# Layer 1's key and query projection as seven half-size products, and two late loads, in a four-layer transformer kernel on one core

## Chip, core and metric

The kernel runs on one core of a Trainium2 chip. The core has a matrix engine (TensorE: PE, with its weight loads shown as PEld), a vector engine (VectorE: DVE), an activation engine (ScalarE: ACT), a general one (GpSimd: POOL) and a queue engine (SyncE: SP); SP and POOL start the DMA transfers here. The metric is the time of one execution on the device in microseconds.

## The reference

Four residual layers follow each other on x of shape (4, 1024, 256), all in float32: attention A, a feed-forward network, attention B, and the same feed-forward network again.

```python
x = x + attn_a(layernorm(x), kernel, WO)      # layer 1
x = x + ffn(layernorm(x), w1, b1, w2, b2)
x = x + attn_b(layernorm(x), ...)             # low rank, with rotation
x = x + ffn(layernorm(x), w1, b1, w2, b2)

def attn_a(x, kernel, WO):                    # 16 heads of 64
    q, k, v = (einsum('bsm,hmd->bhsd', x, kernel[i]) for i in range(3))
    scores = einsum('bhsd,bhtd->bhst', q, k) * (1 / (64 * 64 * 16))
    out = einsum('bhst,bhtd->bhsd', softmax(scores), v)
    return out.transpose(0, 2, 3, 1).reshape(b, s, 1024) @ WO[0]
```

## The kernel before

Everything is written in a hand-made order. Both attentions share `attention`. Work goes by pairs: a pair is one of 4 batches and one of 8 couples of heads, so there are 32 pairs, and each has 8 steps of 128 query rows, 256 steps in all. In a step s the loop `steps_with` emits, engine by engine in this order: `invert(s)` (the reciprocal of the row sums on DVE, L268, and its copy on ACT, L269); `scores(s + 1)` (PE, L247: eight matmuls into two PSUM tiles j = 0 and 1 of 128x1024); on even steps the pT sends of POOL (L304) and `project` (PE by L176; ACT copies the result as `got`, L335; POOL adds it to x, L337); `exponentials(s + 1, 0)` (row maximum on DVE, L258; exponential with row sum on ACT, L260); the pieces that are due half a step early; on odd steps `weigh` (PE, L313); `exponentials(s + 1, 1)`; on odd steps `take` (ACT copies, L323, POOL's product, L325); `turn(s)` (DVE transposes 32x32 blocks into T, L280); on odd steps the pT sends of SP (L304, eleven per two steps, the POOL queue sends five); and last the pieces due at s.

PSUM has two pools. `ps_sc` has three tiles of 128x1024, which the scores take in rotation, two per step, so that a tile waits for the exponential that reads the one three places before it. `ps_mm` has two banks, which `group` hands out in turn for everything else: projections, values, output projection, weighted sums.

The keys and queries of a pair are made during the pair before. `pair_a` gives the pieces: `qk(i, qb)` makes the keys (i = 1) or queries (i = 0) of 512 rows, by `paired` (L176): two accumulated blocks of the 256 input features, each as two matmuls side by side that fill 64 partitions. Each call takes one bank from `group`, and ACT copies it out (L758 for keys; L756 for queries, with the scale). The four calls lie in the even steps 0, 2, 4 and 6 of the pair before, due half a step early, which puts their ACT copy between the two exponentials of the step. `values(m)` (PE, L185; ACT copy, L769) fills four even steps too. `batch_a` prepares the next batch: normalized rows `xn` (L156), turned by PE against the identity (L162) and copied to `hT` by ACT (L165).

The weights of a pair come by POOL's queue (L742) some five steps before they are used. `load_rest` loads at the start the other batches of x (SP's queue), and by POOL's queue both FFN matrices, biases, the low-rank weights of layer 3 and the rotation's tables (four transfers). The FFN's `weights` makes combinations of w1 (DVE) and w2 (POOL) once per network: its middle blocks use Strassen's scheme already (`up_seven`, `down_seven`), the first and the last block use plain products (`up`, `down`). `rotate` (L870 to L872) reads the tables in layer 3.

Of the kernel before, what the change touches and what calls it, by code (L numbers as in the profile page):

```python
# [15 lines left out]
P = 128  # L16
# [3 lines left out]
NC = D // P  # L20
# [28 lines left out]
def hybrid_block_kernel(  # L49
# [24 lines left out]
    pp, tp, ptp, otp, tmp = pool("p", 2), pool("T", 2), pool("pT", 2), pool("oT", 1), pool("tmp", 1)  # L74
    lowp, highp, xnp, rp = pool("low", 2), pool("high", 1), pool("xn", 1), pool("rope", 1)
    qkp, vp, wp, wop = pool("qk", 2), pool("v", 2), pool("wp", 2), pool("wo", 2)

# [15 lines left out]
    w1_sb = const.tile([P, NC, F], F32, name="w1_sb")  # L93
    w2_sb = const.tile([P, NF, D], F32, name="w2_sb")
    b2_sb = const.tile([P, D], F32, name="b2_sb")
    wd_sb = const.tile([P, 2, NC, P], F32, name="wd_sb")
    cos_sb = const.tile([P, S], F32, name="cos_sb")
    sin_sb = const.tile([P, S], F32, name="sin_sb")

    def load_rest():  # L100
        for b in range(1, B):
            nc.sync.dma_start(xs[b], xv[b])
        nc.gpsimd.dma_start(w1_sb, w1.rearrange("(c p) f -> p c f", p=P))
        nc.gpsimd.dma_start(w2_sb, w2.rearrange("(c p) d -> p c d", p=P))
        nc.gpsimd.dma_start(b2_sb, b2.partition_broadcast(P))
        for i, w in enumerate((wdq, wdkv)):
            nc.gpsimd.dma_start(wd_sb[:, i], w.rearrange("(c p) r -> p c r", p=P))
        for j in range(2):
            nc.gpsimd.dma_start(cos_sb[j * DH : (j + 1) * DH, :], rope_cos)
            nc.gpsimd.dma_start(sin_sb[j * DH : (j + 1) * DH, :], rope_sin)  # L110
        nc.gpsimd.dma_start(b1_sb, b1.rearrange("(c p) -> p c", p=P))
        nc.gpsimd.dma_start(lns_sb, ln_s.rearrange("(c p) -> p c", p=P))
        nc.gpsimd.dma_start(lnb_sb, ln_b.rearrange("(c p) -> p c", p=P))


# [41 lines left out]

    def transposed(dst, src, c, affine=None):

        tr = group(TQ, P)  # L160
        for t in range(TQ):
            nc.tensor.transpose(tr[:, t, :], src[:, t, ts(c, P)], ident)  # L162
        trf = tr.rearrange("p t q -> p (t q)")
        if affine is None:
            nc.scalar.copy(dst[:, c, :], trf)  # L165
        else:
            nc.scalar.activation(
                dst[:, c, :], trf, AF.Identity,
                scale=affine[0][:, c : c + 1], bias=affine[1][:, c : c + 1],
            )  # L170
# [224 lines left out]
    def ffn(rows, store):  # L395
# [31 lines left out]
        def weights():  # L427

            wc = ptp.tile([P, SENT], F32, tag="pT", name="wc")
            s1 = wc[:, : 4 * hf * P].rearrange("p (s f) -> p s f", s=4)  # L430
            s2 = wc[:, 4 * hf * P : 8 * hf * P].rearrange("p (s f d) -> p s f d", s=4, f=hf)
            m = hf * P
            parts["w1"] = (s1, w1_sb[:, 0, :m], w1_sb[:, 1, :m], w1_sb[:, 1, m:])
            lo, hi = w2_sb[:, :hf], w2_sb[:, hf:]
            parts["w2"] = (s2, lo[:, :, :P], hi[:, :, :P], hi[:, :, P:])
            v = nc.vector
            work = four([s1[:, i] for i in range(4)], w1_sb[:, 0, :m], w1_sb[:, 1, :m], w1_sb[:, 0, m:], w1_sb[:, 1, m:], [v] * 4)
            work += other([s2[:, i] for i in range(4)], lo[:, :, :P], lo[:, :, P:], hi[:, :, :P], hi[:, :, P:], [nc.gpsimd] * 4)
            for f in work:
                f()  # L440
# [113 lines left out]
        def down_seven(n, hook):  # L554
            b, qb = blocks[n]
            t4, b11, b21, b22 = parts["w2"]
            s, g = sums.pop(n), gT[n]
            a11, a12, a22 = g[:, :hf, :half], g[:, hf:, :half], g[:, hf:, half:]
            pairs = {
                1: (a11, b11), 2: (a12, b21), 3: (s[:, 3], b22), 4: (a22, t4[:, 3]),  # L560
                5: (s[:, 0], t4[:, 0]), 6: (s[:, 1], t4[:, 1]), 7: (s[:, 2], t4[:, 2]),
            }
# [4 lines left out]
            def product(bank, k, first):  # L567
                l, r = pairs[k]
                product_of(bank, lambda t, f: l[:, f, ts(t, P)], lambda f: r[:, f], first, hf)

# [39 lines left out]
        def down(n, t):  # L610
# [3 lines left out]
            for f in range(NF):  # L614
                nc.tensor.matmul(  # L615
                    po[n][:, t % 2, :], gT[n][:, f, ts(t, P)], w2_sb[:, f, :],
                    start=(f == 0), stop=(f == NF - 1),
                )
# [9 lines left out]
    def ffn_between(rows, store, n_steps, nxt=None, prologue=(), ramp=None):  # L628
# [11 lines left out]
        ends += [(n - 1 + (0, 0, 0, 1, 2, 2, 3, 3)[f], lambda f=f: up(0, f)) for f in range(NF)]  # L640
        ends += [(n, lambda: normed(1))]
        ends += [(n + 1, lambda m=m, t=t: rows.measure(m, t)) for m in range(2, 6) for t in range(TQ)]
        ends += [(n + 2, lambda: rows.finish[1]()), (n + 2, weights), (n + 3, lambda: turned(1))]
        ends += [(n + 3, lambda: row_sums(1)), (n + 4, lambda: down(0, 0))]

        def rest():
# [3 lines left out]
            for m in range(1, last + 1):  # L650
# [11 lines left out]
                if m == 1:  # L662
                    for i in range(2 * TQ):
                        when(2 + i, lambda i=i: rows.measure(6 + i // TQ, i % TQ))
                if nxt and m >= 2:
                    for t in range(TQ):
# [38 lines left out]
    def layer_a():  # L705

        scale_a = 1.0 / (DH * DH * H)
        hTs = {}
        rows = Rows("a", (blocks[:1], blocks[1:2], blocks[2:]))

        def batch_a(b):
            work = []
            for qb in range(NQB):
# [12 lines left out]
                def turned(c, b=b, k=k, qb=qb):  # L726
                    if c == 0:
                        p, tag = ((lowp, "low"), (highp, f"high{b % 2}"))[qb]
                        hTs[b, qb] = p.tile([P, NC, QB], F32, tag=tag, name="hT")
                    transposed(hTs[b, qb], k["xn"], c)  # L730

                work += [(10 * qb + t, lambda t=t, f=straight: f(t)) for t in range(TQ)]
                work += [(10 * qb + 6 + 2 * c, lambda c=c, f=turned: f(c)) for c in range(NC)]
            return work

        def pair_a(b, pr):
# [9 lines left out]
            def qk(i, qb):  # L746
# [6 lines left out]
                ])  # L753
                dst = made[name][:, ts(qb, QB)]
                if i == 0:
                    nc.scalar.mul(dst, pq, scale_a)  # L756
                else:
                    nc.scalar.copy(dst, pq)  # L758

            def values(m):  # L760
# [3 lines left out]
                for t in range(4):  # L764
# [3 lines left out]
                    ])  # L768
                nc.scalar.copy(made["v"][:, ts(m, 4), :], pv)  # L769

            work = [(4 - 4 * i + 2 * qb - EARLY, lambda i=i, qb=qb: qk(i, qb)) for i in (1, 0) for qb in range(NQB)]
            work += [(6 + 2 * m, lambda m=m: values(m)) for m in range(NT // 2)]
# [18 lines left out]
        first = loads + [lambda: measured(0)] + xn[:4] + [lambda: measured(1), ready] + xn[4:6] + pair[:1]  # L791
        first += xn[6:] + pair[1:3]
        later += [((-1, 0, 0, 1, 1)[i], f) for i, f in enumerate(pair[3:])]
# [3 lines left out]
    def layer_b(rows):  # L797
# [45 lines left out]
        def pair_b(b, pr):  # L843
# [23 lines left out]
            def rotate(i, qb):  # L867

                straight, other = made[i, qb], turned.pop((i, qb))
                nc.gpsimd.tensor_mul(straight, straight, cos_sb[:, ts(qb, QB)])  # L870
                nc.gpsimd.tensor_mul(other, other, sin_sb[:, ts(qb, QB)])  # L871
                nc.gpsimd.tensor_add(straight, straight, other)  # L872
# [96 lines left out]
```

## Time and profile before

| | |
|---|---|
| median of 3 runs | 3253.09 us (3245.43 to 3254.13) |
| the profiled execution | 3250.15 us, its span 3248.4 us |
| busy over the span | PE 3164.4, PEld 2092.2, DVE 2723.5, ACT 2137.9, POOL 2002.1 us |
| layer 1 | from the start to about 1406 us |
| first FFN | up to about 1800 us, under the start of layer 3 |
| key and query projections of layer 1 | L176 mm<-hT,w, 1024 records (two for each float32 matmul), 243.4 us, 597 ns each |

A line of the profile's timeline has the start and the length in us, the engine, the line of the kernel, the operation, the tile it writes and the tiles it reads, the shapes, and the count of merged instructions; in brackets the idle time of the engine before it and what ended it. A name without its number stands for all buffers of that tile: `sc` are scores, `p` the exponentials, `T` and `pT` their transposed forms, `mm` any tile of `ps_mm`. A matmul's time can contain waiting, because matmuls are pipelined and their ends are modelled. The chain of waits follows the work that ended last back in time; a wait for several semaphores is put down to the one that came last.

### The profile page before, as it was taken

What the parts mean: (1) busy time and instruction counts of PE and PEld (TensorE: products, weight loads), DVE (VectorE), ACT (ScalarE), POOL (GpSimd) and SP (SyncE); (2) the same over time, 40 slices, a digit from 0 to 9 for tenths busy, and PEclk for the clock granted to TensorE, in tenths of its full rate; (3) what the DMA queues carried; (4) which work ended last, traced back from release to release, by engine and by line L of the source; (5) the groups of instructions that cost most, each with busy time, mean ns of one, the idle gap of its engine ahead of it and who ended that gap; (6) DMA issues with size and microseconds to landing.
All of it is one profiled execution on the core that took longest, in us unless ns stands there. A gap on an engine that the chain in (4) does not pass through costs nothing.

```text
span 3248.4 us, 128967 instructions
## 1 busy us (share of the span) xinstructions
PE 3164.4 (97%) x53648; PEld 2092.2 (64%) x53648; DVE 2723.5 (84%) x2686; ACT 2137.9 (66%) x4400; POOL 2002.1 (62%) x2782
## 2 busy tenths in 40 slices
PE   8999999999999999999999999999999999999999
PEld 4666666666666666668866566666666666655688
DVE  7988888888888888966569989998999999999554
ACT  5666666666666666655447777777778777777542
POOL 4544545455444545442249889899899889886311
PEclk9999999999999999999999999999999999999999
DMA  8888888888888888850029889988989899988200
GB/s 228 217 224 215 224 224 228 217 219 222 221 217 225 219 231 223 221 150 1 4 74 244 225 228 243 242 237 236 246 243 243 234 240 246 238 235 221 57 20 27
DMA packets 244709, 642.29 MB, mean 198 GB/s; under 512 B 74304, under 2 KB 102976, under 8 KB 244128
## 3 DMA queue, kind: packets, MB, share of 16 engines
q1 hardware_dynamic: 161104, 397.60, 48.0%
q0 software_dynamic: 83024, 236.44, 26.0%
q8 instruction: 426, 6.98, 1.0%
q14 instruction: 155, 1.27, 0.1%
HBM read 43.39 MB, written 4.19 MB: 15 GB/s over the span
## 4 chain that ended last, share of the span: by engine, by line
PE 69%; SPq 12%; DMA 6%; DVE 5%; ACT 4%; issue 3%; POOL 1%; DVEq 0%; ACTq 0%; POOLq 0%
PE sc L247 20%; PE mm L313 19%; PE mm L176 15%; SPq L304 11%; DMA pT<-T 5%; PE pw L495 4%; PE mm L185 4%; PE mm L495 3%; PE mm L615 2%; DVE T L280 2%; DVE nmax L258 1%; ACT p L260 1%; PE ph L604 1%; ACT gT L529 1%; PE mm L162 1%
## 5 line engine op out<-in xcount | busy, mean ns | idle before, releaser
L258 DVE TENSOR_REDUCE nmax<-sc 128x1 f32<-128x1024 f32 x1024 | 1204.5, 1218 | 214.3 <-PE sc L247 211.3
L260 ACT ACTIVATE p<-sc,nmax 128x1024 f32<-128x1024 f32 x1024 | 1145.3, 1119 | 322.3 <-DVE nmax L258 322.2
L280 DVE STREAM_TRANSPOSE T<-p 128x2176 f32<-128x2176 f32 x512 | 1247.3, 2436 | 48.4 <-DMA pT<-T 18.4
L247 PE MATMUL sc<-kT,qT 64*64 64x512 f32 x8192 | 1082.5, 598 | 11.9 <-ACT p L260 10.3
L313 PEld LDWEIGHTS mm<-pT,v 64*64 64x64 f32 x32768 | 949.5, 133 | 140.7 <-issue 98.5
L313 PE MATMUL mm<-pT,v 64*64 64x128 f32 x32768 | 983.0, 269 | 9.6 <-issue 8.5
L304 POOL DMA_DIRECT2D pT<-T x1280 | 629.6, 499 | 125.5 <-PE sc L247 57.7
L325 POOL TENSOR_TENSOR oT<-oT,pT 128x256 f32<-128x256 f32 x256 | 187.0, 730 | 696.3 <-ACT oT L323 623.0
L247 PEld LDWEIGHTS sc<-kT,qT 64*64 64x64 f32 x8192 | 332.8, 133 | 401.6 <-issue 274.5
L337 POOL TENSOR_TENSOR x<-x,got 128x512 f32<-128x512 f32 x256 | 331.0, 1293 | 25.8 <-ACT got L335 22.0
L335 ACT COPY got<-mm 128x512 f32<-128x512 f32 x256 | 150.0, 586 | 281.8 <-PE mm L176 281.8
L176 PE MATMUL mm<-wo,oT 128*64 128x256 f32 x2048 | 279.9, 394 | 24.1 <-POOL oT L325 22.8
L176 PEld LDWEIGHTS mm<-wo,oT 128*64 128x64 f32 x2048 | 124.9, 136 | 273.2 <-POOL oT L325 226.5
L269 ACT COPY p<-total 128x128 f32<-128x128 f32 x512 | 151.9, 297 | 198.6 <-DVE total L268 192.4
L176 PE MATMUL mm<-hT,w 128*64 128x512 f32 x1024 | 243.4, 597 | 0.9 <-ACT hT L165 0.9
L260 ACT ACTIVATION_READ_ACCUMULATOR p<-sc,nmax 128x1 f32 x1024 | 205.2, 200 | 0.0
L185 PEld LDWEIGHTS mm<-w,hT 128*64 128x64 f32 x4096 | 140.9, 138 | 71.3 <-issue 69.4
L871 POOL TENSOR_TENSOR turned<-turned,sin_sb 128x512 f32<-128x512 f32 x128 | 163.8, 1279 | 0.0
L409 POOL TENSOR_TENSOR x<-x,b_sb 128x256 f32<-128x256 f32 x64 | 48.8, 777 | 170.6 <-ACT xn L156 170.6
L296 ACT COPY pT<-T 32x1088 f32<-32x1088 f32 x128 | 140.3, 1096 | 4.9 <-DMA pT<-T 1.1
L185 PE MATMUL mm<-w,hT 128*64 128x64 f32 x4096 | 140.9, 222 | 0.2 <-ACT kT L758 0.2
L176 PEld LDWEIGHTS mm<-hT,w 128*64 128x64 f32 x1024 | 73.3, 138 | 96.8 <-issue 75.0
(145 smaller groups left out, 2928.5 us busy)
## 6 DMA issues: line engine op xcount, KB each, us to landing
pT<-T SPq DMA_DIRECT2D x2688, 136.0 KB, 4.7
pT<-T POOLq DMA_DIRECT2D x1280, 136.0 KB, 4.7
turned<-kT POOLq DMA_DIRECT2D x128, 128.0 KB, 3.4
turned<-qT POOLq DMA_DIRECT2D x128, 128.0 KB, 3.5
w<-in_wqkv_a POOLq DMA_DIRECT2D x96, 128.0 KB, 6.0
wo<-in_wo_a POOLq DMA_DIRECT2D x32, 128.0 KB, 5.4
wo<-in_wo_a POOLq DMA_DIRECT2D x64, 64.0 KB, 5.5
wo<-in_wo_b SPq DMA_DIRECT2D x32, 128.0 KB, 4.0
```

Of the source, the lines that this page charges most:

```text
L176: nc.tensor.matmul(out[ts(j, DH)], lhsT[:, ts(j, DH)], rhs[j], start=(first and i == 0), stop=(last and i == len(parts) - 1),)
L185: nc.tensor.matmul(out[ts(j, DH)], lhsT, rhs[:, ts(j, DH)], start=(i == 0), stop=(i == len(parts) - 1),)
L247: nc.tensor.matmul(sc[s, j][ts(half, DH), ts(m, 512)], qT()[rows, ts(2 * qs + half, DH)], kT()[rows, ts(m, 512)], start=True, stop=True,)
L258: nc.vector.tensor_reduce(nmax, sc[s, j], AX.X, ALU.max, negate=True)
L260: nc.scalar.activation(probs[s][:, :NK2, ts(j, 2), :], sc.pop((s, j)).rearrange("p (k c i) -> p k c i", c=2, i=SQ), AF.Exp, bias=nmax, acc ...
L280: nc.vector.transpose(T[h][:, :, q, :, :].rearrange("p c k i -> p k c i"), probs.pop(s))
L304: engine.dma_start(pT[h][ts(c, SQ), a], T[h][ts(a, SQ), c])
L313: nc.tensor.matmul(av[h][q][ts(j ^ q, DH)], v[ts(j, DH), k, :], pT[h][ts(j, DH), :, q, k, :], start=(k == 0), stop=(k == NK2 - 1),)
L325: nc.gpsimd.tensor_mul(parts, parts, pT.pop(h)[:, :, :, NK2, :])
L337: nc.gpsimd.tensor_add(xd, xd, got)
L495: nc.tensor.matmul(bank[:, t, : right(k).shape[-1]], left(t, k), right(k), start=(first and t == 0 and k == 0), stop=(k == n_k - 1), skip_ ...
L871: nc.gpsimd.tensor_mul(other, other, sin_sb[:, ts(qb, QB)])
```

## The change

Layer 1 makes the keys and queries of a pair together as one product of two by two blocks: the two blocks of 256 features on one side, queries and keys on the other, and the two halves of the 1024 rows as the columns. Strassen's scheme (in Winograd's form) needs seven half products in place of eight. Each half product is one `paired` call with one block of features, 128x512.

- `row_sums` makes four differences of hT blocks per batch (DVE, 128x512), in steps 21 to 24 of the batch's preparation; for the first batch at the start.
- `weight_sums` makes four combinations of the weights per pair (POOL, 128x128), at the end of the step before the first products.
- `products` runs in the even steps 0, 2, 4, 6, half a step early, where `qk` was: products (1, 6), then (7, 5), then (4, 2), each couple in one tile of `ps_sc`, one bank each; then product 3 alone in a bank of `group`. Each call has one ACT copy: product 1 to x1, product 5 to the upper keys, product 2 to the lower queries, product 3 to the upper queries.
- `added` runs at the end of the same steps: a sum from PSUM on DVE in the first three (u2, u3, the lower keys), and on POOL no sum, two, one and one (128x512).
- The first pair keeps `qk`. The scale of the scores moves: hT is scaled by 1/256 as ACT copies it, and the values are scaled back by 256 in their copy.
- w2 comes in four parts of 256 KB by SP's queue in steps 250 to 253 of layer 1; the rotation's tables by SP's queue in the first FFN (block 1, last hook). The tables' and w2's room holds the row sums, the weight sums, x1, u2 and u3 before that. `weights` sums w2 in eight POOL operations in place of four.

```diff
+    tail = pool("tail", 1)
...
-    w2_sb = const.tile([P, NF, D], F32, name="w2_sb")
-    cos_sb = const.tile([P, S], F32, name="cos_sb")
-    sin_sb = const.tile([P, S], F32, name="sin_sb")
+    def load_w2(i):
+        held["w2", i] = tail.tile([P, 2, D], F32, tag=f"w2{i}", name="w2_sb")
+        rows = w2.rearrange("(c p) d -> p c d", p=P)
+        nc.sync.dma_start(held["w2", i], rows[:, ts(i, 2), :])
+    def load_rope():
+        for name, table in (("cos", rope_cos), ("sin", rope_sin)):
+            held[name] = tail.tile([P, S], F32, tag=name, name=name)
+            for j in range(2):
+                nc.sync.dma_start(held[name][j * DH : (j + 1) * DH, :], table)
...
+        if nxt:
+            ends += [(n - 6 + i, lambda i=i: load_w2(i)) for i in range(4)]
...
+                    if nxt:
+                        when(20, load_rope)
...
-        scale_a = 1.0 / (DH * DH * H)
+        root = 1.0 / DH / H**0.5
...
-                    transposed(hTs[b, qb], k["xn"], c)
+                    transposed(hTs[b, qb], k["xn"], c, scale=root)
...
+            if b:
+                work += [(21 + i, lambda i=i: row_sums(b, i)) for i in range(4)]
...
+        def row_sums(b, i):
+            if i == 0:
+                sums[b] = [tail.tile([P, 2, QB], F32, tag=t, name="hs") for t in ("cos", "sin")]
+            t = [sums[b][k // 2][:, k % 2] for k in range(4)]
+            h = [[hTs[b, qb][:, c, :] for qb in range(NQB)] for c in range(NC)]
+            left, right = ((h[0][1], h[0][0]), (h[1][1], t[0]), (h[1][1], h[0][1]), (h[1][0], t[1]))[i]
+            nc.vector.tensor_sub(t[i], left, right)
...
-                dst = made[name][:, ts(qb, QB)]
-                if i == 0:
-                    nc.scalar.mul(dst, pq, scale_a)
+                nc.scalar.copy(made[name][:, ts(qb, QB)], pq)
+            def weight_sums():
+                s = made["s"] = tail.tile([P, 4, P], F32, tag="w20", name="ws")
+                (q0, q1), (k0, k1) = [[made["w"][:, i, c, :] for c in range(NC)] for i in range(2)]
+                nc.gpsimd.tensor_add(s[:, 0], k0, k1)
+                nc.gpsimd.tensor_sub(s[:, 1], s[:, 0], q0)
+                nc.gpsimd.tensor_sub(s[:, 2], q0, k0)
+                nc.gpsimd.tensor_sub(s[:, 3], q1, s[:, 1])
+            def products(which):
+                w, s, t = made["w"], made["s"], [sums[b][k // 2][:, k % 2] for k in range(4)]
+                h = [[hTs[b, qb][:, c, :] for qb in range(NQB)] for c in range(NC)]
+                sides = {
+                    1: (w[:, 0, 0], h[0][0]), 2: (w[:, 0, 1], h[1][0]), 3: (s[:, 3], h[1][1]),
+                    4: (w[:, 1, 1], t[3]), 5: (s[:, 0], t[0]), 6: (s[:, 1], t[1]), 7: (s[:, 2], t[2]),
+                }
+                if which == (3,):
+                    made[3] = group(QB)
+                else:
+                    both = ps_sc.tile([P, 2, QB], F32, tag="sc", name="pw")
+                    for i, k in enumerate(which):
+                        made[k] = both[:, i]
+                for k in which:
+                    l, r = sides[k]
+                    paired(made[k], [(l, [r] * 2)])
+                if which == (1, 6):
+                    made["x1"] = tail.tile([P, QB], F32, tag="w21", name="x1")
+                    nc.scalar.copy(made["x1"], made[1])
+                elif which == (7, 5):
+                    made["kT"] = qkp.tile([P, S], F32, tag="kT", name="kT")
+                    nc.scalar.copy(made["kT"][:, QB:], made[5])
+                elif which == (4, 2):
+                    made["qT"] = qkp.tile([P, S], F32, tag="qT", name="qT")
+                    nc.scalar.copy(made["qT"][:, :QB], made[2])
                 else:
-                    nc.scalar.copy(dst, pq)
+                    nc.scalar.copy(made["qT"][:, QB:], made[3])
+            def added(which):
+                q, k = made.get("qT"), made.get("kT")
+                if which == (1, 6):
+                    made["u2"] = tail.tile([P, QB], F32, tag="w22", name="u2")
+                    nc.vector.tensor_add(made["u2"], made[6], made["x1"])
+                elif which == (7, 5):
+                    made["u3"] = tail.tile([P, QB], F32, tag="w23", name="u3")
+                    nc.vector.tensor_add(made["u3"], made[7], made["u2"])
+                    nc.gpsimd.tensor_add(made["u2"], made["u2"], k[:, QB:])
+                    nc.gpsimd.tensor_add(k[:, QB:], k[:, QB:], made["u3"])
+                elif which == (4, 2):
+                    nc.vector.tensor_add(k[:, :QB], made[4], made["u3"])
+                    nc.gpsimd.tensor_add(q[:, :QB], q[:, :QB], made["x1"])
+                else:
+                    nc.gpsimd.tensor_add(q[:, QB:], q[:, QB:], made["u2"])
...
-                nc.scalar.copy(made["v"][:, ts(m, 4), :], pv)
-
-            work = [(4 - 4 * i + 2 * qb - EARLY, lambda i=i, qb=qb: qk(i, qb)) for i in (1, 0) for qb in range(NQB)]
+                nc.scalar.mul(made["v"][:, ts(m, 4), :], pv, 1.0 / root)
+
+            if b == 0 and pr == 0:
+                work = [(0, lambda i=i, qb=qb: qk(i, qb)) for i in (1, 0) for qb in range(NQB)]
+            else:
+                work = [(-1, weight_sums)]
+                for i, which in enumerate(((1, 6), (7, 5), (4, 2), (3,))):
+                    work += [(2 * i - EARLY, lambda which=which: products(which))]
+                    work += [(2 * i, lambda which=which: added(which))]
```

## The prediction

> **What bounds the kernel now.** The change works on layer 1, the first 1406 us, so I read that stage alone. First the busy time of each engine in stretches (columns: stretch, its length, busy us and instruction count of PE, PEld, DVE, ACT, POOL, then PE clock, DMA share, GB/s):
>
> ```profile
> 500.00:1000.00 500.00, 498.00 (x9518) 314.56 (x9518) 433.39 (x364) 324.53 (x706) 247.02 (x386) 1.00 0.86 221
> ```
>
> PE is busy 498 of 500 us at full clock. Then the chain of waits in 700 to 750 us (start, us, what):
>
> ```profile
> 705.25 1.72 PE sc L247 x16
> 706.97 2.73 PE mm L176 x16
> 709.70 0.93 PE mm L185 x32
> 710.63 1.88 PE sc L247 x16
> 712.51 3.49 PE mm L313 x128
> ```
>
> The chain is a closed ring of PE work. An even step is scores, then L176 (output projection and half of a key or query projection), then L185 (values); an odd step is scores, then L313 (weigh). So half a product less should be half a product gained, unless something stands close behind PE. What stands there is read in the timeline of one even step:
>
> ```profile
> 707.02 2.36 DVE L258 TENSOR_REDUCE nmax<-sc 128x1 f32<-128x1024 f32 x2 [0.46 <-PE sc L247]
> 707.81 1.89 PE L176 MATMUL mm<-hT,w 128*64 128x512 f32 x8
> 708.09 0.59 ACT L335 COPY got<-mm 128x512 f32<-128x512 f32 x1 [1.19 <-PE mm L176]
> 708.57 1.12 ACT L260 ACTIVATE p<-sc,nmax 128x1024 f32<-128x1024 f32 x1
> 709.29 2.44 DVE L280 STREAM_TRANSPOSE T<-p 128x2176 f32<-128x2176 f32 x1
> 709.58 0.20 ACT L260 ACTIVATION_READ_ACCUMULATOR p<-sc,nmax 128x1 f32 x1
> 709.75 0.60 ACT L756 ACTIVATE qT<-mm 128x512 f32<-128x512 f32 x1
> 710.24 1.11 ACT L260 ACTIVATE p<-sc,nmax 128x1024 f32<-128x1024 f32 x1
> 710.56 1.95 PE L247 MATMUL sc<-kT,qT 64*64 64x512 f32 x16
> 711.24 0.20 ACT L260 ACTIVATION_READ_ACCUMULATOR p<-sc,nmax 128x1 f32 x1
> 712.56 1.22 DVE L258 TENSOR_REDUCE nmax<-sc 128x1 f32<-128x1024 f32 x1 [0.79 <-PE sc L247]
> ```
>
> The first exponential with its accumulator read ends at 709.78, 0.78 us before the next scores start at 710.56; the second ends at 711.44, which is 0.88 us after that start. The same distance lies behind almost every projection: of 121 even steps from 60 us on, 108 show 0.87 or 0.88 us and 12 show 0.28 or 0.29 (an extra transposition of the next batch is on PE there). The step takes 5.54 us (712.56 less 707.02, from one L258 to the next).
>
> The last pair has no projection left, and shows what limits a step then:
>
> ```profile
> 1381.76 2.36 DVE L258 TENSOR_REDUCE nmax<-sc 128x1 f32<-128x1024 f32 x2 [0.46 <-PE sc L247]
> 1383.59 2.50 PE L247 MATMUL sc<-kT,qT 64*64 64x512 f32 x13
> 1384.32 0.20 ACT L260 ACTIVATION_READ_ACCUMULATOR p<-sc,nmax 128x1 f32 x1
> 1386.56 1.23 DVE L258 TENSOR_REDUCE nmax<-sc 128x1 f32<-128x1024 f32 x1
> ```
>
> PE has 1.89 us less to do, but the step takes 4.80 us, only 0.74 less: the scores' second matmul needs the slot of the exponential that ends at 1384.52. From that end to the next L258 it is 2.04 us, which I use as the price of "slot released to scores done"; PE still counts as busy while it waits inside.
>
> The Trainium skill (Perfetto Trace Analysis, "Identifying the Most-Contended Engine") warns that matmul busy time is no good measure of PE's headroom, and asks for the weight loads' share: 314.56 of 500 us, 63%. By that rule PE has room and a cut of its work would be worth less than the busy row promises; the last pair's row agrees in sign, and the sum here goes by that row.
>
> **The change, part by part.**
>
> *1. Removed PE work.* A pair had four key/query calls of 1.89 us (8 records each). Seven products in place of eight halves leave three calls of two products and one of a single product, so 0.95 us less per pair, in the fourth even step alone. For 31 pairs (the first keeps the old form). That step still uses the general PSUM pool, and its scores still wait for the first exponential: end 709.78 plus 2.04 is 711.82, so the step is 4.80 us, not 4.59. In 3 of the 31 a transposition covers the wait and the full 0.95 comes. Gain: 28 x 0.74 + 3 x 0.95 = 23.6 us.
>
> *2. The products' PSUM slot.* The three double products leave the general pool and take one of the three slots that the scores rotate through. In the order S1a S1b S2a S2b a tile reuses the one three places back, so S2b waits for S1a's exponential. With the product W between, S1a S1b W S2a S2b, S2a waits for S1a and S2b for S1b: for the second exponential. ACT reads in the same order as before: copy of got, first exponential, copy out of W, second exponential. The copies of the second product in W cannot start before the pair of products ends (709.70 now); the one that copies the first product still finds ACT in the first exponential until 709.78. So the second exponential ends at 711.44 as now, scores are done 2.04 later, at 713.48, and the step grows from 5.54 to 6.46 us: +0.92. Queued behind this on PE: the rest of the scores and the odd step's weigh, that is everything; PE's odd step (5.21 us) has nothing to shorten. 31 x 3 = 93 such steps; 9 have a transposition as cover and pay 0.33 (252.63 + 2.04 against 254.34 in the step at 250 us); the three of the second pair lie in the start-up, where scores already wait for exponentials: 0 to 0.92 each, I take 0.46. Cost: 81 x 0.92 + 9 x 0.33 + 3 x 0.46 = 78.9 us.
>
> *3. DVE.* One PSUM sum per double product, 128x512; the nearest row is the FFN's L535, 688 ns. It is queued after the transposition, and the next L258 after it: 711.73 + 0.69 + 0.13 (reciprocal L268) = 712.55, before 713.48. Cost nothing; without the cover it is 93 x 0.69 = 64 us. A batch's four row subtractions (by L420, 693 ns) fall in four steps; an odd one pushes L258 by at most 0.7 us, against 0.37 of slack before the first exponential: 0 to 2 us over the run, taken as nothing.
>
> *4. POOL.* Per pair four sums of 128x512 (L337, 1293 ns: 5.2 us) and four of 128x128 (by the step from L325, 730 ns for 256 elements, to 1293 for 512, an estimate of 0.45 us each: 1.8 us). POOL is busy 247 of 500 us, 21.2 of 43 per pair, so 28.2 of about 45. The weight sums start behind an odd step's L325 and push five pT sends and one x sum back by about 1.8 us; those pT blocks are read three steps later (16 us, against 4.7 us to landing). The sums on q and k end before the step that first reads them: the last (upper half of q) lands some 5 us into its step, and those columns are read only from the next pair's fifth step on. Cost nothing; if the sends came late, at most 31 x 1.8 = 56 us.
>
> The Trainium skill (SBUF — State Buffer, "SBUF: two separate sides") says that GpSimd and a VectorE operation with two SBUF inputs lock each other out for a whole instruction. By it only the row subtractions could collide, 16 x 0.69 = 11 us at most. In the stretch 2000 to 2800 us DVE is busy 733.77 and POOL 723.63 us of 800, so they overlap for at least 657; that row has none of these subtractions, and the sum takes nothing.
>
> *5. ACT.* Four copies before and after, 0.59 us; the scale moves from L756 to the copies of hT and v, of like size. Nothing.
>
> *6. Late loads.* 2 MB leave POOL's opening queue (five issues of 0.5 to 0.9 us): PE's start follows x, w and hT (first matmul at 8.93 behind ACT's xn), so no gain. Four 256 KB loads of w2 go to SP's queue in the last steps of the layer, between pT sends that fill it (37 sends in 35.4 us near 1360 us, 0.96 each). One, 0.5 to 1.2 us, stands ahead of the sends for the third-last weigh, where PE already waits 1.11 us at 1409.8; the later ones have 5 us of room. I take +1.2, bounds 0 and 5. The tables load in the FFN at DMA share 0.00 (1450 to 1500 us), and the w2 sums become eight POOL operations of about 0.73 in place of four of 1.27: +0.8 us off the path.
>
> **Sum:** 78.9 - 23.6 + 1.2 = +56.5 us. The profiled execution is 3250.15 us (span 3248.4 and 1.75 around it): 3306.7. It is 2.9 under the median of 3253.09, against which the same sum gives 3309.6. I say 3308.
>
> **Rivals.** (a) *The slot costs nothing*, faster. PE's removed work would come free, 3250.15 - 23.6 + 1.2 = 3228. For it: PE fills 498 of 500 us and the ring holds no ACT. Against: 108 of 121 steps end the second exponential 0.88 us too late; it needs ACT to finish that much earlier. (b) *It cancels*: at 0.25 us for each of the 90 steps gain and loss meet, 3250 to 3256; nothing shows such a price except the 9 covered steps. (c) *DVE or POOL also land on the path*: DVE's sums uncovered (+64) give 3371, late sends (+56) 3363. For it: DVE is already at 433 of 500 us; against: 0.93 us of idle in just the step that gets the sum, and a longer period that eases every other queue. It decides once the sum starts more than 0.93 us late.
>
> **How the numbers follow.** Forecast 0.86, (a) 0.05, (b) 0.03, (c) 0.06. The forecast's own range: the slot's price 0.8 to 1.0 us (81 steps: -10, +6), start-up -1.4 to +1.4, w2 -1.2 to +4, subtractions 0 to 2, the base 3245 to 3254: 3288 to 3326. Leaving (a) out and reaching a little toward (c): 3286 to 3332. About 0.3% (10 us) is what a measurement can tell from no change. Faster 0.05, same 0.03, slower 0.92.
>
> **What would show it.** PE records L176 with pw: even steps of 6.4 to 6.5 us from L258 to L258 three times per pair and 4.8 once, odd ones 5.2; a pair near 45.0 us in place of 43.0; waits of PE's sc for ACT's p; layer 1 ending some 55 us later and everything after it unchanged. It is wrong if the double-product steps stay at 5.5 us (then (a)), or if DVE's L280 or L258 wait for the new sums or pT (then (c)).

## The result, and the profile after

The changed kernel takes 3307.19 us (median of 4 runs, 3302.87 to 3311.1) against 3252.49 us of the kernel before (4 runs, 3245.43 to 3254.13): ratio 1.0164, 95% interval 1.015 to 1.0178. It is slower, by 54.7 us. The forecast was 3308 us.

The same stretch as before, busy time by engine (columns as there), shows PE hardly less busy (498.00 us before) with 425 matmul records fewer:

```profile
500.00:1000.00 500.00, 497.21 (x9093) 318.01 (x9094) 439.00 (x389) 310.28 (x675) 309.88 (x459) 1.00 0.82 212
```

The busy row alone hides the loss. The timeline of one even step with two products (product 4 and 2) shows it; between the two L271 lies the step:

```profile
1421.37 2.36 DVE L271 TENSOR_REDUCE nmax<-sc 128x1 f32<-128x1024 f32 x2 [0.32 <-PE sc L260]
...
1424.09 0.59 ACT L826 COPY qT<-pw 128x512 f32<-128x512 f32 x1
1424.58 1.12 ACT L273 ACTIVATE p<-sc,nmax 128x1024 f32<-128x1024 f32 x1
...
1424.91 2.44 PE L260 MATMUL sc<-kT,qT 64*64 64x512 f32 x13
...
1425.58 0.20 ACT L273 ACTIVATION_READ_ACCUMULATOR p<-sc,nmax 128x1 f32 x1
...
1425.84 0.21 PEld L260 LDWEIGHTS sc<-kT,qT 64*64 64x64 f32 x8 [0.74 <-ACT p L273]
1426.00 0.65 DVE L843 TENSOR_TENSOR kT<-pw,u 128x512 f32<-128x512 f32 x1
...
1427.82 2.35 DVE L271 TENSOR_REDUCE nmax<-sc 128x1 f32<-128x1024 f32 x2 [1.10 <-PE sc L260]
```

The step takes 6.45 us (1427.82 less 1421.37). PE's weight load for the scores sat idle 0.74 us until ACT had read the second exponential's sum, at 1425.78; from there to the next L271 it is 2.04 us, the same 2.04 as in the forecast. The matmul beside it counts 2.44 us as busy in place of 1.95: the wait lies inside. DVE then waited 1.10 us for the scores, so its sum (1426.00) delayed nothing.

The waits of 100 to 1400 us, added up (engine, line, what it waited for, us in total, times, longest), have a new entry, the first line here (2.8 us in 3 waits before); the second line was 11.6 us in 3 waits before:

```profile
PEld sc L260 <- ACT p L273: 58.7, 86, 0.9
POOL oT L338 <- DMA pT<-T: 58.4, 23, 2.6
```

For a table by step I took all 256 steps from one L271 (L258 before) to the next and compared each with the same step of the kernel before. The three even steps with two products lie at 6.45, 6.46 and 6.47 us (5.54 before) and cost 79.2 us over the layer; the even step with one product lies at 4.81 and gains 19.4; the odd steps stay at 5.21, but the one after the single product is at 5.36 and costs 2.1. From the first to the last of these lines layer 1 takes 1449.4 us in place of 1388.6, 60.8 more. What lies behind it took 1827.2 us in this execution and 1835.3 in the one before; it took 1844.4 and 1848.7 us in profiled executions of two kernels that change nothing there (slot alone, and slot read late), so no gain is read from it.

### The profile page after: what moved, and what is told of

Read it like the earlier page. It is cut to its first block, busy times and chain, and to the rows that moved or that the text cites. A ratio compares the mean times of both kernels' runs of the same rounds, so it can differ in the third digit from the quotient of the medians.

```text
span 3300.9 us, 129026 instructions
## 1 busy us (share of the span) xinstructions
PE 3214.2 (97%) x53524; PEld 2131.9 (65%) x53524; DVE 2790.2 (85%) x2795; ACT 2138.2 (65%) x4400; POOL 2205.1 (67%) x3033
## 4 chain that ended last, share of the span: by engine, by line
PE 68%; SPq 11%; DMA 6%; DVE 6%; ACT 4%; issue 3%; POOL 1%; DVEq 0%; POOLq 0%; ACTq 0%
PE sc L260 21%; PE mm L326 18%; SPq L317 11%; PE mm L189 9%; DMA pT<-T 6%; PE pw L189 4%; PE pw L513 4%; PE mm L198 4%; PE mm L513 3%; DVE T L293 2%; DVE nmax L271 2%; PE mm L634 2%; ACT p L273 1%; PE ph L623 1%; ACT gT L547 1%
## 5 line engine op out<-in xcount | busy, mean ns | idle before, releaser
L271 DVE TENSOR_REDUCE nmax<-sc 128x1 f32<-128x1024 f32 x1024 | 1204.3, 1218 | 203.6 <-PE sc L260 200.5
L260 PE MATMUL sc<-kT,qT 64*64 64x512 f32 x8192 | 1193.4, 598 | 17.4 <-ACT p L273 13.0
L326 PEld LDWEIGHTS mm<-pT,v 64*64 64x64 f32 x32768 | 995.0, 133 | 116.1 <-issue 101.8
L326 PE MATMUL mm<-pT,v 64*64 64x128 f32 x32768 | 1035.9, 269 | 6.8 <-issue 4.7
L260 PEld LDWEIGHTS sc<-kT,qT 64*64 64x64 f32 x8192 | 383.6, 132 | 453.7 <-issue 256.1
L189 PE MATMUL mm<-wo,oT 128*64 128x256 f32 x2048 | 277.5, 392 | 23.6 <-POOL oT L338 22.6
L965 POOL TENSOR_TENSOR turned<-turned,sin 128x512 f32<-128x512 f32 x128 | 163.8, 1279 | 0.0
L189 PE MATMUL mm<-hc,w 128*64 128x512 f32 x512 | 132.9, 597 | 0.0
L336 ACT COPY oT<-mm 128x128 f32<-128x128 f32 x512 | 110.3, 268 | 10.3 <-PE mm L326 10.2
```

The costliest lines, as they stand in the source:

```text
L189: nc.tensor.matmul(out[ts(j, DH)], lhsT[:, ts(j, DH)], rhs[j], start=(first and i == 0), stop=(last and i == len(parts) - 1),)
L260: nc.tensor.matmul(sc[s, j][ts(half, DH), ts(m, 512)], qT()[rows, ts(2 * qs + half, DH)], kT()[rows, ts(m, 512)], start=True, stop=True,)
L271: nc.vector.tensor_reduce(nmax, sc[s, j], AX.X, ALU.max, negate=True)
L326: nc.tensor.matmul(av[h][q][ts(j ^ q, DH)], v[ts(j, DH), k, :], pT[h][ts(j, DH), :, q, k, :], start=(k == 0), stop=(k == NK2 - 1),)
L965: nc.gpsimd.tensor_mul(other, other, held["sin"][:, ts(qb, QB)])
```

## The experiments

All results first (steps are medians; kernels without double products have the same steps of a pair listed; "layer" is the difference of layer 1 to the kernel before, whose own length moved by up to 3.7 us between executions with equal steps; a ratio is to the kernel before on the same chip):

| kernel | steps with two products | step with one | layer, us | median, us | ratio, interval |
|---|---|---|---|---|---|
| before | 5.54 5.54 5.54 | 5.54 | | 3252.49 | |
| changed | 6.45 6.46 6.47 | 4.81 | +60.8 | 3307.19 | 1.0164 (1.015, 1.0178) |
| slot alone | 5.54 5.54 5.54 | 5.54 | +3.4 | 3257.91 | 1.0006 (0.9995, 1.0016) |
| slot, read late | 6.45 6.46 6.46 | 5.55 | +79.3 | 3344.46 | 1.0281 (1.026, 1.0303) |
| sums left out | 5.53 5.54 6.45 | 4.81 | +16.7 | 3275.27 | 1.0059 (1.0044, 1.0075) |
| copies late | 6.12 5.90 5.90 | 5.16 | +20.6 | 3267.33 | 1.0032 (1.0021, 1.0044) |
| got late too | 6.11 5.63 5.63 | 5.05 | +9.2 | 3259.65 | 1.0009 (0.9998, 1.002) |
| sends moved | 6.08 5.63 5.63 | 4.94 | +23.9 | 3275.6 | 1.0057 (1.0043, 1.0071) |
| weight sums moved | 6.18 5.63 5.63 | 4.83 | +13.0 | 3272.99 | 1.0052 (1.0036, 1.0068) |
| slot freed by ACT | 6.12 5.84 5.84 | 4.81 | +15.7 | 3269.54 | 1.0047 (1.0032, 1.0061) |
| late loads alone | 5.54 5.54 5.54 | 5.54 | +3.7 | 3252.64, one run | |
| sum before exponential | 6.52 6.40 7.53 | 4.80 | +90.7 | 3344.3 | 1.0283 (1.0263, 1.0303) |
| same order, sum late | 6.45 6.46 7.53 | 4.82 | +110.5 | 3367.01, one run | |
| sum apart | 5.54 5.54 5.78 | 5.18 | +3.4 | 3250.64 | 0.9978 (0.9965, 0.9991) |

### The slot alone

The kernel before, but three of a pair's four key and query calls take a tile of the scores' pool:

```diff
-                pq = group(QB)
+                if (b, pr) != (0, 0) and (i, qb) != (0, 1):
+                    pq = ps_sc.tile([P, 2, QB], F32, tag="sc", name="pw")[:, 0]
+                else:
+                    pq = group(QB)
```

> The kernel before, with one part of the change alone: three of the four key and query calls of each pair (all but the fourth) take their PSUM tile from the scores' rotation instead of the general pool. No Strassen product, no new sum, no late load. Slot theory: the double-product steps' price without their gain, 5.54 becomes 6.46 three times per pair: 3252 + 79 = 3331 us. Theory of the new sums or of the late loads: no change, 3252 us.

It costs nothing, so the reason in the forecast falls as it was worded: a tile between the scores does not by itself move their wait. Its timeline of an even step:

```profile
708.53 1.89 PE L176 MATMUL pw<-hT,w 128*64 128x512 f32 x8
...
710.46 0.60 ACT L759 ACTIVATE qT<-pw 128x512 f32<-128x512 f32 x1
710.96 1.11 ACT L260 ACTIVATE p<-sc,nmax 128x1024 f32<-128x1024 f32 x1
...
711.28 1.95 PE L247 MATMUL sc<-kT,qT 64*64 64x512 f32 x16
...
711.96 0.20 ACT L260 ACTIVATION_READ_ACCUMULATOR p<-sc,nmax 128x1 f32 x1
...
713.27 1.23 DVE L258 TENSOR_REDUCE nmax<-sc 128x1 f32<-128x1024 f32 x1 [0.79 <-PE sc L247]
```

The scores run 1.95 us with no wait inside, from 0.88 us before the second exponential's end (712.16). The only reader of the projection's tile, the copy at 710.46, stands on ACT ahead of that exponential. In the changed kernel the last reader is DVE's sum, written at the end of the step, behind it. This gave a second theory: slots go out in the order in which their last readers stand in the program, and S2b gets W's slot if W's last reader stands ahead of the second exponential, but that exponential's own slot if it stands behind.

### The sums left out

The changed kernel without weight sums (the weights themselves stand in), u2, u3 and all of POOL's sums; of DVE's sums only the one in the third double step stays:

```diff
-                if which == (1, 6):
...
-                elif which == (4, 2):
-                    nc.vector.tensor_add(k[:, :QB], made[4], made["u3"])
...
+                if which == (4, 2):
+                    nc.vector.tensor_add(k[:, :QB], made[4], made["x1"])
```

> The changed kernel without most of its new sums: the four weight sums per pair, the four sums on POOL and two of the three sums on DVE are left out (raw weights stand in for the sums), products, copies, row sums and PSUM slots stay. Slot theory: the sums are covered, only 0.15 us per pair of the weight sums and the like come back: 3300 to 3307 us. Theory of the new sums: up to 64 us (DVE) or 56 us (POOL) less, 3245 to 3265 us.

Neither band was hit (1.0059, 3275.27 us), and the steps say why: two double steps without a sum take 5.53 and 5.54 us, the third, which kept its sum, 6.45. Strict rotation would make all three 6.45; a price of DVE's time is not met either, since 0.65 us of sum cost 0.91. The place of the last reader fits all three.

### The slot, with a tiny read at the end of the step

The slot alone, plus a DVE reduction of two columns of W where the change has its sum:

```diff
+                    nc.vector.tensor_reduce(seen, pq[:, :2], AX.X, ALU.max)
```

> The kernel before, with the slot of the run e3_slot_alone, and one tiny read added: at the end of each such step, where the changed kernel has its DVE sum, DVE reads two columns of the projection's PSUM tile (128x2, about 0.1 us). Refined theory (the slot costs only while its last reader is ordered behind the second exponential, because the scores' second tile then takes the slot which that exponential frees): double-product steps go from 5.54 to 6.46 us, 84 of them: 77 us more, ratio about 1.024. Theory that the DVE sum's own time or the POOL sums cost: no change, ratio 1.000 to 1.003.

The whole cost is back, with all of the old PE work:

```profile
735.50 1.12 ACT L260 ACTIVATE p<-sc,nmax 128x1024 f32<-128x1024 f32 x1
...
735.83 2.44 PE L247 MATMUL sc<-kT,qT 64*64 64x512 f32 x13
736.50 0.20 ACT L260 ACTIVATION_READ_ACCUMULATOR p<-sc,nmax 128x1 f32 x1
...
736.91 0.12 DVE L768 TENSOR_REDUCE seen<-pw 128x1 f32<-128x2 f32 x1
...
738.74 2.36 DVE L258 TENSOR_REDUCE nmax<-sc 128x1 f32<-128x1024 f32 x2 [1.64 <-PE sc L247]
```

The read takes 0.12 us and ends at 737.03; a wait for it would give 737.03 plus 2.04, 739.07. L258 starts at 738.74, which is 2.04 behind the second exponential (736.70). So the scores do not wait for the reader; the reader's place decides which slot they get. Over the layer the three steps lose 79.6 us, as much as in the changed kernel.

### The second exponential brought forward

Two kernels keep the late sum and move ACT's work instead: first the copies out of W behind the second exponential (copies late), then the copy of `got` too, in three of four even steps (got late too).

```diff
+            def copied(which):
                 if which == (1, 6):
                     made["x1"] = tail.tile([P, QB], F32, tag="w21", name="x1")
                     nc.scalar.copy(made["x1"], made[1])
...
             def added(which):
+                copied(which)
```

```diff
+                    taken = project(h)
+                    late = ahead and kept == 0 and s % NT != 6
+                    if not late:
+                        taken()
...
                     exponentials(s + 1, 1)
+                if late:
+                    taken()
```

> The changed kernel with one thing moved: the ACT copies out of the three double products come after the second exponential of their step, at the end of the step, instead of between the two exponentials. Slot theory (the scores' second tile waits for the second exponential): that exponential then ends 1.10 us after the first (709.78 + 1.10 = 710.88 on the clock of the step in the prediction), scores are done 2.04 later, so a double-product step is 5.90 us instead of 6.46; 81 x 0.56 + 9 x 0.33 + 0.5 = 49 us less than 3307: 3258 us. Theory that the new sums on DVE and POOL are the cost: the copies' place doesn't matter, 3307 or a little more, because x1 comes later.

> As the run before, and ACT's copy of the output projection (got) also moves behind the second exponential, in all even steps of layer 1 but a pair's fourth (there the values wait for its bank). Slot theory: the first exponential starts when its maximum is there, 1.2 us after the first L258 instead of 1.55, and the second right behind it, ending 3.66 us after that L258; plus 2.04 makes a double-product step 5.70 us; 84 x 0.2 = 17 us less than the run before: about 3240 us, faster than the kernel before the change. Theory of the new sums: no change against 3307, or slower, since the x sum on POOL comes later.

One copy of 0.59 us fewer ahead of the second exponential takes 0.56 us off the second and third double steps (6.46 to 5.90, as expected), two take 0.83 off (5.63). The totals, 3267.33 and 3259.65 us, miss the expected 3258 and 3240, and the first double step keeps 6.1 us. The late copy of x1 does not explain that: in the second kernel the first DVE sum waits for it only 7 times, 1.8 us in all. The second kernel equals the kernel before, not better: it also loses 6 us of the single step's gain, and shows who is late next. In a timeline line, DVE's transposition finds its target buffer T still being sent:

```profile
462.74 2.44 DVE L293 STREAM_TRANSPOSE T<-p 128x2176 f32<-128x2176 f32 x1 [1.47 <-DMA pT<-T]
```

Its sums of waits of 100 to 1400 us have the same cause twice (in the kernel before, these are 11.6 us for POOL's product and 9.2 for DVE's transposition):

```profile
POOL oT L338 <- DMA pT<-T: 83.3, 31, 5.6
...
DVE T L293 <- DMA pT<-T: 19.2, 23, 2.4
```

Two attempts to relieve that, built on this kernel with x1 copied early, failed. One gives POOL six of the sixteen sends in place of five:

```diff
-                    send(s // HB - 1, nc.gpsimd, sent[len(sent) - POOL_DMA :])
+                    send(s // HB - 1, nc.gpsimd, sent[len(sent) - by_pool :])
```

> The run e2_got_late_too with two more moves: in a pair's first step the copy to x1 comes right behind the second exponential, so that the first DVE sum doesn't wait for it, and in layer 1 POOL sends six of the sixteen pT blocks instead of five, SP ten instead of eleven. If the two left-over costs of that run are the late x1 (first step 6.11 us against 5.63) and SP's full queue (fourth step 5.05 against 4.80), the steps become about 5.65 and 4.80, 14 and 8 us less: ratio to the kernel before about 0.994. If POOL has no room for the sixth send, its sums come late and the ratio stays at 1.000 or above.

The other keeps five and puts the weight sums half a step earlier, ahead of POOL's oT product (`-1 - EARLY` for `-1`):

> The run e6_tuned with POOL back at five sends and the four weight sums moved ahead of POOL's product for oT in the same step, where POOL idled for over 2 us. If the weight sums behind that product are what makes the pT sends and so the next transposition late, the first odd step falls from 5.36 to 5.21 and the first even step from 6.1 to about 5.65; ratio 0.995 to 0.999. If POOL's load as a whole is the limit, it stays at 1.001 or above.

Both are worse than the kernel before (1.0057 and 1.0052). With x1 copied early the first double step still takes 6.08 and 6.18 us, not the expected 5.65, so the late x1 was not its cost; with the weight sums earlier the first odd step stays at 5.36. POOL's product still waits for pT (61.2 and 69.5 us). Which of POOL's load, the queues and the landing of pT sets this limit stays open.

### The slot freed by ACT

ACT copies both products of W between the two exponentials, and DVE adds from SBUF. W's last reader then stands ahead of the second exponential, which itself comes 0.48 us later (3.70 us after the step's first L271 in place of 3.22).

```diff
+                    nc.scalar.copy(made["u2"], made[6])
...
-                    nc.vector.tensor_add(made["u2"], made[6], made["x1"])
+                    nc.vector.tensor_add(made["u2"], made["u2"], made["x1"])
```

> The changed kernel with the PSUM tile of the double products freed before the second exponential: ACT copies both products (two copies of 0.59 us in place of one) and the DVE sums read the copies, at the same place as before. Refined theory (what costs is that the tile's last reader is ordered behind the second exponential): the scores' second tile gets the products' slot, free at about 3.9 us after the step's first L271, plus 2.0 makes 5.9 us in place of 6.46, although ACT does half a microsecond more: some 45 us less than the changed kernel, ratio to the kernel before 1.002 to 1.006; should two SBUF inputs slow the DVE sums (the row differences took up to 1.35 us), up to 0.3 us per step are lost again, 1.009. Theory that any extra slot in the rotation costs: no change, 1.016.

5.84 in place of 6.46, though ACT works longer; the ratio of 1.0047 lies in the second theory's band.

### The late loads alone

The kernel before with the four w2 loads in SP's queue in the last steps of layer 1 and the tables in the FFN.

> The kernel before with the late loads alone: w2 by SP's queue in steps 250 to 253, the tables in the first FFN. By the prediction's sixth term 1.2 us more in the last two pairs' steps (bounds 0 and 5), nothing elsewhere; if the loads are a cost of their own it shows as longer steps after 1395 us.

The last ten steps of the layer, in which the loads start, are those of the kernel before to 0.03 us; the one run takes 3252.64 us, where the kernel before lies between 3251.23 and 3264.68. The loads cost nothing that can be measured.

### The sum ahead of the second exponential

If the second theory is right, the cure is not to hurry ACT but to move DVE's sum: behind the second row maximum and ahead of the transposition. The products are taken in another order, in which each sum needs one product from PSUM and one older tile. The second kernel is its control.

```diff
-                for i, which in enumerate(((1, 6), (7, 5), (4, 2), (3,))):
+                for i, which in enumerate(((1,), (6, 5), (7, 2), (4, 3))):
...
             nc.vector.tensor_reduce(nmax, sc[s, j], AX.X, ALU.max, negate=True)
+            while j and between:
+                between.pop()()
             nc.scalar.activation(
```

> All seven products stay, in another order: product 1 alone in the first even step, then (6, 5), (7, 2), (4, 3), so that each double product needs one DVE sum whose other input is an earlier SBUF tile. That sum stands right behind the second row maximum, ahead of the second exponential and of the transposition. Release-order theory: both readers of W (ACT copy, DVE sum) now come before the second exponential in program order, so the scores' second tile takes W's slot and no longer waits for that exponential: the three double steps fall from 6.45 to 5.54-5.75 us, the step with product 1 alone takes 4.8-5.0. DVE's transposition starts 0.7-1.0 us later, which may push the next row maximum by up to 0.4 us: +0 to +0.2 us per double step. Ratio 0.993 to 0.999 (3230 to 3250 us). Rotation theory (any tile between moves the wait) and the theory that DVE's sums themselves cost: double steps stay at 6.4 us or more, ratio 1.016.

> The control: the order of the products as in the run before it, but the DVE sum back at the end of the step, behind the second exponential. Release-order theory: the three double steps at 6.4 to 6.5 us again, the single one at 4.8, about 3300 us. If the new order of products alone gives the gain: 5.5 to 5.8 us and about 3240 us.

The control does what it should in the first two double steps (6.45, 6.46). The other misses: 6.52 and 6.40, not 5.5 to 5.75. Its timeline:

```profile
711.97 0.58 ACT L830 COPY qT<-pw 128x512 f32<-128x512 f32 x1
...
712.45 1.12 ACT L276 ACTIVATE p<-sc,nmax 128x1024 f32<-128x1024 f32 x1
712.59 0.69 DVE L841 TENSOR_TENSOR u<-pw,u 128x512 f32<-128x512 f32 x1 [1.03 <-ACT qT L830]
```

The sum reads product 7 and waits 1.03 us for ACT's copy of product 2. No data pass between them; both read the same PSUM tile. In the trace each of the 31 sums of this line carries a wait for ACT; the same sum in the kernel of the next section, where its product is alone in its tile, carries none. The transposition behind it is late by as much, and DVE, which then had no idle left, sets the step (it comes to the next row maximum at 715.60). Besides, both kernels finish the lower queries on POOL a step too late for the next pair (the third step's 7.53 us): a fault of the edit, not of the theory.

### The sum apart

Both faults mended: the product that DVE sums is alone in its tile of the scores' pool, the one that ACT copies goes to a bank of `group`, and the lower queries' sum stands one even step earlier.

```diff
-                    both = ps_sc.tile([P, 2, QB], F32, tag="sc", name="pw")
-                    for i, k in enumerate(which):
-                        made[k] = both[:, i]
+                for k in which:
+                    made[k] = group(QB) if k in (1, 5, 2, 3) else ps_sc.tile(
+                        [P, 2, QB], F32, tag="sc", name="pw")[:, 0]
```

> The two faults that the run with the sum ahead of the second exponential showed are mended: the DVE sum waited for the ACT copy of the other product of its tile (1.0 us a step), and the lower queries' sum on POOL came too late for the next pair's first scores (2 us a pair). Now only the product that DVE sums lies in the scores' pool, alone in its tile; the one that ACT copies lies in a bank of the general pool; the lower queries' sum stands at the end of the third even step. W's only reader is the DVE sum, ahead of the second exponential. Release-order theory: its slot goes to the scores' second tile and is free 0.7 us earlier than that exponential, so the three double steps take 5.55 to 5.75 us, the single one 4.8 to 4.85, odd ones as before but the first (5.35). Sum over 31 pairs: -15 to -17, +3 to +5, +3 to +20: ratio 0.995 to 1.002 (3237 to 3260 us). Theory that DVE's sums are the cost wherever they stand: DVE's next row maximum is pushed by the whole 0.65 us, double steps at 6.1 us or more, ratio 1.012 or more.

All seven products, and 3250.64 us against 3257.8 of the kernel before on the same chip: ratio 0.9978, the interval just clear of 1. The timeline of a double step:

```profile
712.68 0.68 DVE L838 TENSOR_TENSOR u<-pw,u 128x512 f32<-128x512 f32 x1
...
713.28 2.44 DVE L296 STREAM_TRANSPOSE T<-p 128x2176 f32<-128x2176 f32 x1
713.62 1.12 ACT L276 ACTIVATE p<-sc,nmax 128x1024 f32<-128x1024 f32 x1
713.95 1.95 PE L261 MATMUL sc<-kT,qT 64*64 64x512 f32 x16
...
714.63 0.20 ACT L276 ACTIVATION_READ_ACCUMULATOR p<-sc,nmax 128x1 f32 x1
...
715.95 2.36 DVE L272 TENSOR_REDUCE nmax<-sc 128x1 f32<-128x1024 f32 x2 [0.19 <-PE sc L261]
```

The second exponential ends at 714.83, again 0.88 us after the scores' start, and again it does not matter: 1.95 us, a step of 5.54. Each instruction in a trace carries the waits that the program gave it. Those of the first weight load for each of the two score tiles behind a double product agree (engine waited for). The first wait is for the first exponential in both; the second is for ACT in the changed kernel and for DVE, that is for the sum, here:

```
changed:    L260 sc<-kT,qT [waits Activation]   L260 sc<-kT,qT [waits Activation]
sum apart:  L261 sc<-kT,qT [waits Activation]   L261 sc<-kT,qT [waits DVE]
```

The other runs with a tile W agree too. In the first two double steps of a pair the second wait is for DVE in the two kernels with the sum ahead of the second exponential (58 and 55 of 58 steps in 29 pairs); in all the others it is for ACT (49 to 58 of the 58, in the control all).

The gain is small. The single step is back at 5.18 (in the one at 731.93 us the transposition waits 0.49 us for ACT), and the third double step scatters from 5.54 to 6.99 with two of 8.89 and 10.06. The profiled execution is also the slowest of its ten (3257.52), so where the 7 us of the median lie is not seen in it.

## Why the prediction was right, and where it was not

*The sum and the sign.* +56.5 us were forecast, +54.7 came, at 3307.19 for 3308. That it came this close is in part luck: in the profiled executions layer 1 lost 60.8 us, 4.3 more than the sum, and what lies behind it came out 8.1 us shorter, inside its scatter. The terms of the forecast's own range add up to about 3289 to 3324 us, not 3288 to 3326; the result lies inside both.

*The slot's price* was right to the second digit: 0.92 a step and 78.9 us were worked out, 0.91 to 0.93 and 79.2 came, with 2.04 us from the exponential's end to the next row maximum in both kernels. The wait named, "S2b for S1b", is the one in the trace.

*The slot's reason* failed: "a tile reuses the one three places back … With the product W between … S2a waits for S1a and S2b for S1b". By that the slot alone would have cost the same. It costs nothing (1.0006), and the same slot with 0.12 us of reading at the end of the step costs all (1.0281). Which slot S2b gets depends on whether W's last reader stands ahead of the second exponential. That the slots go out in order of release is inferred: it fits the double steps of the kernels above and the waits that their score loads carry. The price came out right by luck: the change happens to have a late reader, which the prediction does not name as the reason. For the same reason its rival (a) was argued wrongly, "it needs ACT to finish that much earlier": in the last kernel ACT finishes no earlier, and the slot costs nothing.

*The removed product* was sized too high. Of 23.6 us, 19.4 came in the single steps, and the odd steps behind them gave 2.1 back. Most single steps are at the forecast's 4.80, but "its scores still wait for the first exponential" is at most one reason of three. In the one at 884.82 us that exponential ends at 887.59, and the scores start at 887.61 and run 1.97 us. But the values ahead of them had waited 0.76 us, until 886.53, for ACT's copy of `got` (22.1 us in 29 waits from 100 to 1400 us; 0.3 us in one wait before), and so end only there as well; and DVE's maximum, transposition and reciprocal (2.36, 2.43 and 0.12) fill the step too. No run separates the three. And a step with a transposition of the next batch gains 0.24 (6.12 to 5.88), not "the full 0.95", because a new wait takes the cover's place (timeline of the changed kernel):

```profile
248.69 0.59 ACT L828 COPY qT<-mm 128x512 f32<-128x512 f32 x1
...
249.33 0.66 PE L173 MATMUL mm<-ident,xn 128*128 128x128 f32 x4 [0.43 <-ACT qT L828]
```

PE is through with the single product so early that L173 waits for the bank that L828 has still to empty.

*DVE's sums* were covered as said, with 1.10 us of idle left behind the sum shown (0.93 was the estimate). The kernel with 0.12 us of reading has the same 6.46 us steps as the one with 0.65 us of sum, so the sum's length is free there. It is free only while the slot is lost: where DVE was made to wait ahead of it, it set the step.

*POOL* did not reach the path in the changed kernel to a degree that shows in the steps. But "cost nothing" was too simple: its product waited 58.4 us for pT, 11.6 before, under the cover of the longer period. Once the period shrank (got late too), this was the next limit.

*The late loads* (+1.2) are nothing that can be measured. *ACT* at nothing is right in sum, though the place of its copies ahead of the second exponential is worth 0.56 us a step as soon as that exponential is waited for.

## What to carry to other kernels

In a pool whose tiles are handed out as they come free, ask of a new tenant not how long it stays but who reads it last, and where that reader stands in the program against the readers of the others: here 0.12 us of reading in the wrong place cost 79.6 us in the three steps of each pair (the whole kernel 3344.46 us against 3256.48). Let each short-lived PSUM tile have one reader, and put it ahead of the instruction whose slot must not be inherited. And when a forecast comes out to the digit, still test its mechanism alone: the cure (move the reader) followed only from the right one.

## What the runs showed of the hardware

A row subtraction on DVE takes both inputs from SBUF and has lengths from 642 to 1347 ns in the changed kernel. In the kernel with the sum ahead of the exponential (timeline, DVE and POOL):

```profile
732.68 0.70 DVE L772 TENSOR_TENSOR hs<-hT 128x512 f32<-128x512 f32 x1
732.79 0.90 POOL L798 TENSOR_TENSOR ws<-w 128x128 f32<-128x128 f32 x1
...
737.48 1.29 POOL L353 TENSOR_TENSOR x<-x,got 128x512 f32<-128x512 f32 x1
737.98 1.35 DVE L772 TENSOR_TENSOR hs<-hT,hs 128x512 f32<-128x512 f32 x1
```

In the first pair POOL starts second and takes 0.90 us, where the next three weight sums take 0.46: DVE ends at 733.38, 0.59 us into POOL's instruction, which leaves 0.31. In the second DVE starts second: POOL ends at 738.77, 0.79 us into DVE's instruction, and 1.35 less 0.79 leaves 0.56, where the shortest subtraction takes 0.64. Whoever starts second seems to do most of its work only when the other is done.

The Trainium skill (SBUF — State Buffer, "SBUF: two separate sides") says just this of a VectorE operation with two SBUF inputs and a GpSimd operation that reads SBUF: the first to start holds the shared ports for its whole instruction. These rows agree with it, but for remainders that are 0.15 and 0.08 us shorter than the lengths alone. The forecast took nothing for it, with 11 us as its most; with 16 subtractions in all, and odd steps whose sums over the layer moved by 0.3 to 2.1 us, it can have cost a few us at most here.
